# Attention heads: inverting the softmax sums in a reshaped copy, and scaling the results on GpSimd

## The chip, the cores and the metric

One core of a Trainium2 chip. The metric is the time of one execution on the device in microseconds (us), as a median over runs.

## The reference

1250 nodes with 768 features. A graph stage (two GAT layers over 41250 edges, added to the input) is followed by a transformer block: a layer norm, attention over all 1250 nodes with 12 heads of 64, and a mixture of 8 experts of which each node uses two. Everything is float32. The change lies in the attention alone:

```
qkv    = x @ Wqkv                      # 12 heads of 64
scores = q @ k.T * 64**-0.5            # 1250 x 1250 for each head
attn   = softmax(scores)               # exp(s - max) / sum
out    = (attn @ v) @ Wproj
```

## The kernel before

The graph stage, the attention, the projection with routing, and the experts follow each other. The attention runs over 18 *units*: 6 pairs of heads (`p`) times 3 chunks of 417, 417 and 416 queries (`k`). It works on transposed scores: keys on 125 partitions (10 key tiles, `j` = 0 to 9), queries along the free dimension, the two heads of the pair side by side, so that one tile `s` is 125 x 2 x 417.

For a unit, in the order of the data:
- `scores` (L674): TensorE makes the scores of one key tile for both heads (`st`, L678), ScalarE copies them to SBUF (`sT`, L681), VectorE folds them into a running maximum (`most`, L687).
- `top` (L689) and `row` (L698): TensorE transposes the maxima (`ptop`, L694), VectorE reduces them (`m`, L696), and TensorE spreads the result over the partitions (`mb`, L703).
- `weights` (L706): VectorE subtracts the maximum (L708), ScalarE takes the exponential (L709), GpSimd adds the exponentials of the key tiles up in `acc` (L714, two buffers).
- `values` (L716): TensorE multiplies the exponentials with `v` into `pav` (L722): 128 partitions (two heads of 64) by 417 queries.
- `divide` (L733): TensorE sums `acc` over the partitions with a matrix of ones (`pz`, L731), so that all 64 partitions of a head hold the same row of 417 sums. VectorE takes the reciprocal of the whole 128 x 417 tile (`rz`, L737) and multiplies `pav` by it into `aT` (L738).

Units overlap. In the loop (L756 to L788) unit `u` goes through `weights` and `values` while the next unit `nxt` goes through `scores`; the sums of the unit before (`last.divide()`, L769) stand between `u.top()` and `u.row()`. While a pair of heads runs, TensorE also computes the queries and keys of the next pair, in small steps put between the other work (`queries_keys`, L626; matmuls L641, evictions to `qk` by ScalarE, L644). For the last pair there is no next one: units 15, 16 and 17 have no such steps. I call units with such steps *filled*, and units 15 and 16 *plain*. Unit 17, the last, is filled up by the scheduler with the first matmuls of the projection (`po`, L929), and its sums are partly made on TensorE (`ns` = 5).

The order on TensorE inside a unit is as written (`manual_schedule`); the other engines' order is the scheduler's, and `keep_in_program_order` holds an instruction where it is written. Weights for the queries and keys (`wqk`, one buffer, 2 loads of 384 KB for a pair) come through SyncE's queue (L630): the load for the pair after next can only be issued when the last step has read the buffer. The same queue loads half of the rows `xs` (L155, L156) near the end of unit 14, and `first_w` (L843) at the end.

Of the kernel before, what the change touches and what calls it, by code (L numbers as in the profile page):

```python
# [10 lines left out]
F32 = mybir.dt.float32  # L11
# [6 lines left out]
ALU = mybir.AluOpType  # L18
# [9 lines left out]
def gnn_ffn_kernel(  # L28
# [24 lines left out]
    nc = tc.nc  # L53
    N, D = x.shape
    E = src.shape[0]
    P = 128
    T = 125
# [3 lines left out]
    H, HD = 12, 64  # L61
# [28 lines left out]
    CW = -(-N // NCK)  # L90
# [4 lines left out]
    small = ctx.enter_context(tc.tile_pool(name="small", bufs=3))  # L95
    dram = ctx.enter_context(tc.tile_pool(name="dram", bufs=1, space=bass.MemoryType.DRAM))
    keys = dram.tile([E + SL], F32, name="keys")
    xsd = dram.tile([N, D], F32, name="xsd")
    xd = dram.tile([NE * REG + P, RW], F32, name="xd")

    gate = ctx.enter_context(tc.tile_pool(name="gate", bufs=1))
# [61 lines left out]
    with tc.tile_pool(name="cnt", bufs=1) as cpool:  # L163
# [53 lines left out]
        with tc.tile_pool(name="edge", bufs=1) as ep, \  # L217
# [160 lines left out]
            for u0 in range(0, NU, 4):  # L378
                n = min(4, NU - u0)
# [224 lines left out]
    aT = attn.tile([P, DC, N], F32, name="aT")  # L604
    with tc.tile_pool(name="att", bufs=2) as ap, \
# [20 lines left out]
        def queries_keys(p):  # L626

            wqk = ap.tile([P, DC, 2, P], F32, tag="wqk", name="wqk", bufs=1)
            for i in (1, 0):
                nc.sync.dma_start(wqk[:, :, i, :], Wqkv[:, i * D + p * P:i * D + (p + 1) * P].rearrange(  # L630
                    "(c p) f -> p c f", p=P))
            qk = ap.tile([P, 2, N], F32, tag="qk", name="qk")
            yield qk
            for c0, w in CHUNKS:
                for i in (1, 0):
                    if i == 1:
                        pq = apm.tile([P, 2, 512], F32, tag="mb", name="pk")[:, 0, :]
                    else:
                        pq = apa.tile([P, 512], F32, tag="pz", name="pq")
                    for c in range(DC):  # L640
                        nc.tensor.matmul(pq[:, :w], wqk[:, c, i, :], yT[:, c, c0:c0 + w],  # L641
                                         start=(c == 0), stop=(c == DC - 1))
                        if c == DC - 1:
                            nc.scalar.mul(qk[:, i, c0:c0 + w], pq[:, :w], 1.0 if i == 1 else HD ** -0.5)  # L644
                        yield None

        def go(steps, n):
            for _ in range(n if steps is not None else 0):
                next(steps, None)
# [12 lines left out]
        onesf = ap.tile([T, HD], F32, name="onesf", bufs=1)  # L662
        nc.vector.memset(onesf, 1.0)

        class Unit:


# [38 lines left out]
            def weights(self, j):  # L706
                w, s = self.w, self.s[j]
                nc.vector.tensor_tensor(s[:, :, :w], s[:, :, :w], self.mb[:T, :, :w], ALU.subtract)  # L708
                nc.scalar.activation(s[:, :, :w], s[:, :, :w], AF.Exp)  # L709
                if j == 1:  # L710
                    self.acc = ap.tile([T, 2, CW], F32, tag="acc", name="acc")
                if 0 < j < self.ns:
                    prev = self.s[0] if j == 1 else self.acc
                    nc.gpsimd.tensor_tensor(self.acc[:, :, :w], prev[:, :, :w], s[:, :, :w], ALU.add)  # L714
# [15 lines left out]
                for i, r in enumerate(heads):  # L730
                    nc.tensor.matmul(self.pz[r, :self.w], onesf, t[:, i, :self.w], start=start, stop=stop)  # L731

            def divide(self):  # L733
                w = self.w
                self.sums(self.acc, self.ns == NT, True)
                rz = ap.tile([P, CW], F32, tag="rz", name="rz", bufs=1)
                nc.vector.reciprocal(rz[:, :w], self.pz[:, :w])  # L737
                nc.vector.tensor_tensor(aT[:, self.p, self.c0:self.c0 + w], self.pav[:, :w], rz[:, :w], ALU.mult)  # L738

        steps = queries_keys(0)  # L740
        qks = [next(steps)]
# [11 lines left out]
                    value_rows(j + BEFORE)  # L753
        units = [(p, k) for p in range(DC) for k in range(NCK)]
        steps = last = None
        for n, (p, k) in enumerate(units):  # L756
            if k == 0:
                steps = None
                if p + 1 < DC:
                    steps = queries_keys(p + 1)  # L760
                    qks.append(next(steps))
            nxt = Unit(*units[n + 1], qks[units[n + 1][0]]) if n + 1 < len(units) else None
            u.ns = NT if nxt is not None else NS
            with tc.manual_schedule(engines={mybir.EngineType.PE}):

                go(steps, 2)
                u.top()
                if last is not None:
                    last.divide()  # L769
                go(steps, DC - 2)  # L770
                if nxt is not None:
                    nxt.scores(0)
                u.row()
                u.weights(0)
                u.weights(1)
                for j in range(0, NT, 2):
                    for i in range(2):
                        if nxt is not None and j + i > 0:
                            nxt.scores(j + i)
                    if j < 6:  # L780
                        go(steps, 2)
                    for i in range(2):
                        if j + i + 2 < NT:
                            u.weights(j + i + 2)
                    for i in range(2):
                        u.values(j + i)
            last, u = u, nxt
        last.divide()  # L788


    pin = tc.keep_in_program_order
# [47 lines left out]
    def load_expert(w, w1s, w2s):  # L839

        w1 = w[:, :DC * FF].rearrange("p (c f) -> p c f", c=DC)
        w2 = w[:, DC * FF:].rearrange("p (c f) -> p c f", c=FC)
        nc.sync.dma_start(w1, w1s)  # L843
        nc.sync.dma_start(w2, w2s)
        return w1, w2

    def expert(e):
        return W1[e].rearrange("(c p) f -> p c f", p=P), W2[e].rearrange("(c p) f -> p c f", p=P)
# [60 lines left out]
    with tc.tile_pool(name="proj", bufs=3, reuse_waits="tile") as pp, \  # L909
# [6 lines left out]
        w = load_expert(first_w, *expert(0))  # L916
# [8 lines left out]
        def product(t):  # L925
            po = ppo.tile([P, 2, 512], F32, tag="po", name="po")
            for s in range(2):
                for c in range(DC):
                    nc.tensor.matmul(po[:T, s, :DH], aT[:, c, t * T:(t + 1) * T],  # L929
                                     wp[:, c, s * DH:(s + 1) * DH],  # L930
                                     start=(c == 0), stop=(c == DC - 1))
                    yield None
            y2 = pp.tile([T, D], F32, tag="y2", name="y2")
            ln_apply(y2, xs[:, t, :], st0[:, 0, t:t + 1], st0[:, 1, t:t + 1])
            o = y2.rearrange("p (s d) -> p s d", s=2)
            nc.vector.tensor_tensor(o, o, po[:T, :, :DH], ALU.add)
            mean, rstd = ln_stats(y2)
            yn = normed[t % len(normed)]
            ln_apply(yn[:T, :D], y2, mean, rstd)
            nc.vector.tensor_add(xs[:, t, :], xs[:, t, :], y2)  # L940
            split_rows(nc.sync if t % 2 == 0 else nc.scalar, out[t * T:(t + 1) * T, :], xs[:, t, :])
            nc.vector.tensor_copy(yn[:T, D:D + 1], number[:, t:t + 1])
            yield yn
# [106 lines left out]
        with tc.manual_schedule(engines={mybir.EngineType.PE}):  # L1050
            a, b = route(NT - 3, yns[NT - 3], tally), product(NT - 1)
# [9 lines left out]
            a, b = (route(t, yns[t], tally) for t in (NT - 2, NT - 1))  # L1061
# [17 lines left out]
    with tc.tile_pool(name="moe", bufs=2, reuse_waits="tile") as mp, \  # L1079
# [41 lines left out]
        for i, (e, n, _, _) in enumerate(jobs):  # L1121
# [6 lines left out]
            if i + 1 < len(jobs):  # L1128
                _, m, ws, slots = jobs[i + 1]
                xr, _ = fetch(slots(), m, pin)  # L1130
                w = load_expert(mp.tile([P, 2 * DC * FF], F32, tag="w", name="we"), *ws)
# [34 lines left out]
```

## Time and profile before

| | us |
|---|---|
| median of 3 runs | 1517.28 (1515.45 to 1519.91) |
| the profiled execution | 1518.66, its span 1516.8 |
| TensorE busy in the span | 1437.4 (95%) |
| VectorE busy | 808.4 (53%) |
| ScalarE, GpSimd busy | 574.4 (38%), 418.4 (28%) |
| reciprocals `rz` (L737) | 18 of 2.76 |
| multiplications into `aT` (L738) | 18 of 0.59 |
| units 0 to 14 end at | 1106.5 |
| unit 15, unit 16 | 1106.47 to 1133.27, 1133.27 to 1159.39 |

The time from one `ptop` to the next is taken as a unit. In a listing by time each line has the start, the time from the first to the last instruction of the group, the engine, the line, the operation, output and input, and the number of instructions; in brackets the idle time of the engine before it and what ended that. PEld is TensorE's weight load, which overlaps its matmuls. A window's row has, for each engine, the busy time and the instructions in it, then the TensorE clock that was granted, the share of the DMA engines' time, and GB/s.

### The profile page before, as it was taken

The page shows a single profiled execution, that of the slowest core. Times are in us where ns is not written, and L with a number is a line of the kernel's source. Part 1 is how long each engine was busy: PE and PEld are TensorE (multiplying, and loading weights), DVE is VectorE, ACT ScalarE, POOL GpSimd, SP SyncE. Part 2 cuts the span into 40 slices and gives each one's busy share as a digit, 9 for nine tenths or more (in the row PEclk, how much of TensorE's full clock was granted, in tenths as well). Part 3 has the DMA queues.
Part 4 walks back from the last instruction along what each step waited for, and adds up shares of the span by engine and source line. Part 5 has one row for each costly group of instructions (what it writes and reads, how often), then busy time and mean ns, then how long its engine had stood idle before and what let it go on. Part 6 is the DMA issues. An engine that isn't in the chain of part 4 may idle for free. (4 is left out here: it accounts for less than half of the span.)

```text
span 1516.8 us, 15936 instructions
## 1 busy us (share of the span) xinstructions
PE 1437.4 (95%) x5990; PEld 784.6 (52%) x5990; DVE 808.4 (53%) x1287; ACT 574.4 (38%) x915; POOL 418.4 (28%) x278
## 2 busy tenths in 40 slices
PE   6787999999999999999999999999988999899997
PEld 4574555556555555553343344344333666665654
DVE  6688456434036650127778778777878654111111
ACT  4220613205116521226646656655656223221211
POOL 5000000000000010006656655665666222222222
PEclk9758999999999999999999999999999998899999
DMA  7000020000021129940000000000030323565653
GB/s 208 22 2 11 11 73 0 0 28 5 3 100 42 60 81 383 373 152 0 22 1 0 22 1 21 1 22 0 4 99 1 134 107 136 215 234 171 229 187 124
DMA packets 48198, 124.58 MB, mean 82 GB/s; under 512 B 5629, under 2 KB 22207, under 8 KB 48120
## 3 DMA queue, kind: packets, MB, share of 16 engines
q1 hardware_dynamic: 31468, 57.35, 11.6%
q0 software_dynamic: 11968, 56.21, 10.2%
q10 hardware_dynamic: 4684, 9.99, 2.2%
q8 instruction: 48, 0.79, 0.2%
q14 instruction: 30, 0.25, 0.0%
HBM read 70.46 MB, written 57.55 MB: 84 GB/s over the span
## 5 line engine op out<-in xcount | busy, mean ns | idle before, releaser
L714 POOL TENSOR_TENSOR acc<-acc,sT 125x834 f32<-125x834 f32 (+1 forms) x139 | 272.9, 1963 | 10.9
L526 PE MATMUL pagg<-h,wt 125*125 125x385 f32 (+1 forms) x800 | 263.5, 486 | 0.4 <-DVE wt L519 0.4
L687 DVE TENSOR_TENSOR most<-most,st 125x834 f32<-125x834 f32 (+1 forms) x144 | 146.9, 1020 | 107.1 <-ACT sT L681 104.2
L526 PEld LDWEIGHTS pagg<-h,wt 125*125 125x125 f32 x800 | 147.0, 187 | 104.7 <-DVE wt L519 3.5
L708 DVE TENSOR_TENSOR sT<-sT,mb 125x834 f32<-125x834 f32 (+1 forms) x180 | 174.1, 1014 | 22.6 <-PE mb L703 22.6
L709 ACT ACTIVATE sT<-sT 125x834 f32<-125x834 f32 (+1 forms) x180 | 158.4, 900 | 49.3 <-DVE sT L708 48.9
L681 ACT COPY sT<-st 125x834 f32<-125x834 f32 (+1 forms) x180 | 151.6, 848 | 53.9 <-PE st L678 52.1
L678 PE MATMUL st<-qk 64*125 64x417 f32 (+1 forms) x720 | 164.8, 558 | 4.0 <-DVE most L687 4.0
L722 PE MATMUL pav<-sT,v 125*64 125x417 f32 (+1 forms) x720 | 151.8, 534 | 9.4 <-ACT sT L709 9.4
L619 POOL MEMSET zero<- 128x771 f32 x1 | 0.7, 740 | 529.7 <-PE ptr L143 529.7
L714 POOL TENSOR_TENSOR acc<-sT 125x834 f32<-125x834 f32 (+1 forms) x18 | 35.4, 1964 | 275.9 <-ACT sT L709 275.9
L678 PEld LDWEIGHTS st<-qk 64*125 64x125 f32 x720 | 56.8, 185 | 99.4 <-issue 43.2
L722 PEld LDWEIGHTS pav<-sT,v 125*64 125x64 f32 x720 | 42.8, 137 | 106.3 <-issue 44.4
L900 PE MATMUL poe<-we,hT 128*128 128x384 f32 x264 | 89.8, 486 | 0.0
L641 PE MATMUL pq<-yT,wqk 128*128 128x417 f32 (+1 forms) x216 | 88.1, 534 | 0.0
L867 PE MATMUL phe<-xT,we 128*128 128x384 f32 (+1 forms) x288 | 86.6, 460 | 0.0
L929 PE MATMUL po<-wp,aT 128*125 128x384 f32 x240 | 86.5, 497 | 0.0
L641 PE MATMUL pk<-yT,wqk 128*128 128x417 f32 (+1 forms) x216 | 84.0, 526 | 0.0
L206 PE MATMUL ph<-gw,xnT 128*125 128x384 f32 x240 | 81.6, 500 | 0.8 <-DMA gw<-in_L_gnn_W_dram 0.8
L657 PE MATMUL pv<-wv,yT 128*125 128x384 f32 x240 | 79.9, 490 | 1.4 <-issue 1.4
L206 PE MATMUL ph<-gw,x1T 128*125 128x384 f32 x240 | 79.2, 491 | 0.0
L530 DVE RECIPROCAL rz<-pagg 125x1 f32<-125x1 f32 x20 | 3.3, 166 | 141.4 <-PE pagg L526 141.4
(225 smaller groups left out, 1718.5 us busy)
## 6 DMA issues: line engine op xcount, KB each, us to landing
xd<-zero POOLq DMA_DIRECT2D x8, 3855.0 KB, 15.7
we<-in_L_ffn_W_dram SPq DMA_DIRECT2D x16, 1152.0 KB
xr<-xd SPq DMA_DIRECT2D x25, 385.5 KB
gw<-in_L_gnn_W_dram SPq DMA_DIRECT2D x2, 2304.0 KB
wqk<-in_L_ffn_Wqkv_dram SPq DMA_DIRECT2D x12, 384.0 KB
xres<-in_x_dram SPq DMA_DIRECT2D x10, 375.0 KB
xsd<-xres ACTq DMA_DIRECT2D x10, 375.0 KB
xn<-in_x_dram SPq DMA_DIRECT2D x9, 336.0 KB
```

The lines of the kernel that those rows point to most:

```text
L206: nc.tensor.matmul(po[:, s, :DH], xT[:, c, t * T:(t + 1) * T], w[:, c, s * DH:(s + 1) * DH], start=(c == 0), stop=(c == DC - 1))
L526: nc.tensor.matmul(po[:, s, :DH + s], ws[j][:, (d - d0) * T:(d - d0 + 1) * T], h[:, j, s * DH:(s + 1) * DH + s], start=(j == 0), stop=(j = ...
L641: nc.tensor.matmul(pq[:, :w], wqk[:, c, i, :], yT[:, c, c0:c0 + w], start=(c == 0), stop=(c == DC - 1))
L678: nc.tensor.matmul(st[:T, i, :w], self.qk[r, 1, j * T:(j + 1) * T], self.qk[r, 0, self.c0:self.c0 + w], start=True, stop=True)
L681: nc.scalar.copy(s[:, :, :w], st[:T, :, :w])
L687: nc.vector.tensor_tensor(self.most[:, :, :w], prev[:, :, :w], st[:T, :, :w], ALU.max)
L708: nc.vector.tensor_tensor(s[:, :, :w], s[:, :, :w], self.mb[:T, :, :w], ALU.subtract)
L709: nc.scalar.activation(s[:, :, :w], s[:, :, :w], AF.Exp)
L714: nc.gpsimd.tensor_tensor(self.acc[:, :, :w], prev[:, :, :w], s[:, :, :w], ALU.add)
L722: nc.tensor.matmul(self.pav[r, :w], v[:, j, hd0:hd0 + HD], s[:, i, :w], start=(j == 0), stop=(j == NT - 1))
L867: nc.tensor.matmul(ph[:, :n * P], w1[:, c, f * P:(f + 1) * P], xT[:, c, :], start=(c == 0), stop=(c == DC - 1))
L900: nc.tensor.matmul(po[:, d, :DH], hT[:, f, s * P:(s + 1) * P], w2[:, f, d * DH:(d + 1) * DH], start=(f == 0), stop=(f == FC - 1))
```

## The change

For 17 of the 18 units, `divide` no longer divides. ScalarE copies the sums to SBUF (`zs`) and the unscaled results to `aT`. Two DMAs write one row of 417 sums for each head to memory (`zd`, padded to 420), and one reads the 840 values back as 120 partitions of 7 columns (`z`). VectorE inverts that tile in the middle of the next unit (`invert`, pinned after the block `j == 4`). One DMA writes the inverses to memory (`zr`), two spread them over 64 partitions each (`rz`, two buffers). At the top of the unit after that, GpSimd multiplies `aT` by `rz` in place (`scale`, pinned). The last unit still divides as before. `acc` gets one buffer in place of two.

```diff
+    ZW = 420
+    zd = dram.tile([3 * H // 2, 2, ZW], F32, name="zd")
+    zr = dram.tile([3 * H // 2, 2, ZW], F32, name="zr")
...
+        zs = ap.tile([P, ZW], F32, name="zs", bufs=1)
+        nc.vector.memset(zs, 1.0)
+        ZQ = 7
+        ZP = 2 * ZW // ZQ
+
+        def inverses(n):
+            return ap.tile([P, ZW], F32, tag="rz", name="rz")
...
-                    self.acc = ap.tile([T, 2, CW], F32, tag="acc", name="acc")
+                    self.acc = ap.tile([T, 2, CW], F32, tag="acc", name="acc", bufs=1)
...
-            def divide(self):
+            def divide(self, n):
                 w = self.w
                 self.sums(self.acc, self.ns == NT, True)
-                rz = ap.tile([P, CW], F32, tag="rz", name="rz", bufs=1)
-                nc.vector.reciprocal(rz[:, :w], self.pz[:, :w])
-                nc.vector.tensor_tensor(aT[:, self.p, self.c0:self.c0 + w], self.pav[:, :w], rz[:, :w], ALU.mult)
+                self.o = aT[:, self.p, self.c0:self.c0 + w]
+                if n + 1 == len(units):
+                    nc.vector.reciprocal(zs[:, :w], self.pz[:, :w])
+                    nc.vector.tensor_tensor(self.o, self.pav[:, :w], zs[:, :w], ALU.mult)
+                    return
+                nc.scalar.copy(zs[:, :w], self.pz[:, :w])
+                nc.scalar.copy(self.o, self.pav[:, :w])
+                for i in range(2):
+                    nc.sync.dma_start(zd[n, i:i + 1, :], zs[i * HD:i * HD + 1, :])
+                self.z = small.tile([ZP, ZQ], F32, tag="z", name="z", bufs=1)
+                nc.sync.dma_start(self.z, zd[n].rearrange("i (a b) -> (i a) b", b=ZQ))
+
+            def invert(self, n):
+                tc.keep_in_program_order(nc.vector.reciprocal(self.z, self.z))
+                nc.sync.dma_start(zr[n].rearrange("i (a b) -> (i a) b", b=ZQ), self.z)
+                self.rz = inverses(n)
+                for i in range(2):
+                    nc.sync.dma_start(self.rz[i * HD:(i + 1) * HD, :], zr[n, i:i + 1, :].to_broadcast([HD, ZW]))
+
+            def scale(self):
+                tc.keep_in_program_order(nc.gpsimd.tensor_tensor(self.o, self.o, self.rz[:, :self.w], ALU.mult))
...
+        waiting = []
...
                 if last is not None:
-                    last.divide()
+                    last.divide(n - 1)
+                for old in waiting:
+                    old.scale()
...
                     for i in range(2):
                         u.values(j + i)
+                    if j == 4 and last is not None:
+                        last.invert(n - 1)
+                        waiting = [last]
             last, u = u, nxt
-        last.divide()
+        last.divide(n)
+        for old in waiting:
+            old.scale()
```

## The prediction

> **What bounds the kernel now.** TensorE is busy for 95% of the span, so I first asked where in the attention it is not. Windows of about one unit each:
>
> ```profile
> 819.00:848.00 29.00, 28.69 (x127) 11.82 (x128) 22.76 (x23) 17.09 (x22) 17.64 (x9) 1.00 0.10 28
> 1107.00:1130.00 23.00, 19.73 (x86) 6.96 (x84) 20.26 (x20) 14.98 (x18) 14.70 (x9) 0.85 0.29 76
> 1130.00:1152.00 22.00, 17.87 (x84) 6.82 (x84) 19.13 (x20) 13.64 (x17) 13.00 (x8) 0.92 0.00 1
> ```
>
> The third number is TensorE, the fifth group VectorE. A filled unit has 28.69 of 29 us on TensorE; what is left is one wait of 0.31 for an exponential. In the plain units TensorE is idle for 3 to 4 us of 22, VectorE is busy for 87 to 88%, and the granted clock is below 1.
>
> Next, what the reciprocal holds up. In a filled unit (VectorE's listing by time):
>
> ```profile
> 820.16 2.76 DVE L737 RECIPROCAL rz<-pz 128x417 f32<-128x417 f32 x1
> 822.95 0.59 DVE L738 TENSOR_TENSOR aT<-pav,rz 128x417 f32<-128x417 f32 x1
> 824.90 2.88 DVE L708 TENSOR_TENSOR sT<-sT,mb 125x832 f32<-125x832 f32 x3 [1.36 <-PE mb L703]
> ```
>
> Both are done 1.36 us before the first subtraction can start, which waits for `mb`, behind TensorE's six steps: they cost nothing there. In unit 15, from the listing of all engines:
>
> ```profile
> 1108.72 2.75 DVE L737 RECIPROCAL rz<-pz 128x416 f32<-128x416 f32 x1
> 1109.24 1.12 PE L703 MATMUL mb<-ident,m 105*125 105x105 f32 x8
> 1111.39 0.96 DVE L708 TENSOR_TENSOR sT<-sT,mb 125x834 f32<-125x834 f32 x1
> 1112.27 0.58 DVE L738 TENSOR_TENSOR aT<-pav,rz 128x416 f32<-128x416 f32 x1
> 1113.34 1.03 PE L722 MATMUL pav<-sT,v 125*64 125x417 f32 x4 [2.08 <-ACT sT L709]
> 1116.35 3.15 PE L678 MATMUL st<-qk 64*125 64x417 f32 x8
> 1119.10 1.02 DVE L687 TENSOR_TENSOR most<-most,st 125x834 f32<-125x834 f32 x1 [0.66 <-ACT sT L681]
> ```
>
> Here `mb` ends at 1110.36 and the subtraction starts at 1111.39: the reciprocal is late. TensorE waits 2.08 us for the first exponential, and then the matmuls of two score tiles take 3.15 us (1.67 in the filled unit), because the clock has fallen:
>
> ```profile
> 1107.00:1114.00 7.00, 4.92 (x30) 2.30 (x28) 6.39 (x6) 2.81 (x4) 0.03 (x1) 1.00 0.93 247
> 1114.00:1121.00 7.00, 6.61 (x20) 2.13 (x20) 6.34 (x8) 5.30 (x7) 5.98 (x4) 0.51 0.01 2
> 1141.00:1145.00 4.00, 3.49 (x12) 1.34 (x12) 4.00 (x5) 2.33 (x4) 3.32 (x2) 0.57 0.01 4
> ```
>
> **What it removes.** 17 reciprocals of 2.76 and 17 multiplications of 0.59 leave VectorE, 57 us of work. In units 1 to 14 they end 1.36 us early, so the gain is 0. Unit 17: after `mb` TensorE runs without a gap (projection matmuls fill it), so 0. Units 15 and 16: with no reciprocal the first subtraction starts about 0.10 after `mb` (as 824.90 against 824.80), at 1110.46 instead of 1111.39: 0.93. The multiplication held 0.50 more between subtractions (1112.27 to 1112.76). Together 1.43 a unit; in unit 16 the same rows read 1138.20, 1139.08 and 1139.58, again 1.43. Two units: 2.86. What follows (exponential, `pav`, the next scores, their copies, the maxima) is a ring in which each waits for the link before, so I let it all move up.
>
> **The clock.** TensorE's idle of 2.08 shrinks to about 1.2, since the first exponential can start at 1111.5, not 1112.38 (in the built order it now also stands ahead of the second score copy). If the clock then stays up, VectorE's idle behind the slow scores goes too: 0.66 above and 0.63 at the same place in unit 16, 1.29 in all. If it falls anyway, 0. Nothing in the trace shows a gap of 1.2 us in a stretch this thin, so I take half, 0.65.
> The Trainium skill, page "TensorE: Matmul & The Clock Gate", section "What's actually happening", has the clock halve only after a whole idle window of about 3.4 us. By that rule a gap of 2.08 would leave it at 1.00 and this term would be 0. The trace shows 0.51 after it; the trace decides.
>
> **What it adds to VectorE.** One reciprocal of 120x7 in the middle of each unit. One-column reciprocals (L132) took 145 to 166 ns, and 417 columns 2758, so 6.6 ns a column: 0.16 to 0.20. In filled units VectorE has idle time at the end of the unit; in the two plain ones it costs 0.4. It waits for `z`, and the unit's last two subtractions are queued behind it. In a filled unit `pz` ends at 819.86; a copy (0.52, the row of L644), two issues (0.46 each, L630), a landing, an issue and a landing lead to `z`. The rows nearest to such small transfers are the indirect ones, 3.1 us to memory and 4.8 from it:
>
> ```profile
> sofar<-out_dram,ids POOLq DMA_INDIRECT x23, 4.8
> out_dram<-sofar,ids POOLq DMA_INDIRECT x23, 3.1
> ```
>
> With 4.8 for both, 831.4; the slot, after the first of three subtractions at 834.23, is 835.2. Covered. In unit 15 the `xs` loads fill the DMA engines until about 1114, so `z` comes at 1118 to 1120, close to its slot at 1120: 0 to 1 us, taken as 0.
>
> **ScalarE** gets two copies of about 0.52 ahead of the `qk` eviction and the first score copy. They wait for `pav` and `pz`, during an idle of 6.93 (filled) and 4.43 (unit 15): 0, and 1.0 if that cover were gone. In unit 15 the `xs` DMA issues stand between them; the first exponential needs its subtraction (1111.42) anyway.
>
> **GpSimd** gets 17 multiplications; 834 columns take 1.96, so 417 about 1.0. They stand before a unit's first addition, where it is idle for 10.6 (filled) or 7.8 (plain), and `rz` landed in the unit before: 0. The chain of nine additions starts with the second exponential and so moves up with it; in unit 16 it ended at 1159.90 and `pz` began at 1160.43, a margin of 0.53. Unit 16's own multiplication comes at about 1177, ahead of the projection tile that needs it (after 1185). `acc` with one buffer: the next first addition (828.47) waits for matmuls that ended at 819.86: 0.
>
> **SyncE** gets 102 DMAs. What is queued behind them: `wqk` at four pair changes, `xs` in unit 14, `first_w` in unit 17 (issued 1179.43, `rz` before that). For `wqk`, from three views (SyncE's queue, windows of 1 us, weight loads):
>
> ```profile
> 837.33 0.96 SPq L630 DMA_DIRECT2D wqk<-in_L_ffn_Wqkv_dram  x2
> 840.00:841.00 1.00, 1.00 (x8) 0.33 (x6) 0.26 (x1) 1.00 (x2) 0.92 (x2) 1.00 1.15 333
> 841.00:842.00 1.00, 1.00 (x8) 0.15 (x4) 0.90 (x2) 0.49 (x1) 1.00 (x1) 1.00 0.34 85
> 845.39 0.30 PEld L641 LDWEIGHTS pk<-yT,wqk 128*128 128x128 f32 x2 [0.65 <-issue]
> ```
>
> Both halves are in by about 841.3, the half needed first by about 840.2, and it is used at 845.39. Now the queue waits for the write of `zr`, then issues two `rz`: 835.4 (slot and reciprocal) + 0.46 + landing 3.1 + 0.92 = 839.9, 2.5 late; with 4.8, 4.2 late. The `rz` themselves move 215 KB, 0.65 at 333 GB/s. The first half is then in by 843.4 to 845.1: hidden at both ends, and I take 0.
> [...]
>
> TensorE's work is unchanged; in unit 17 six instead of nine projection matmuls stand ahead of `pz`, a change of order in a stretch without gaps: 0.
>
> **Sum.** 2.86 + 0.65 - 0.4 = 3.1 us. The profiled execution would go from 1518.66 (span 1516.8 and 1.9 around it) to 1515.6. It was 1.4 above the median of the runs, so I take the gain off the median: 1517.28 - 3.1 = 1514.2.
>
> **Rivals.** What this kernel's measurement can tell from no change is about 0.3%, 4.55 us: below 1512.7 is faster, above 1521.8 slower.
> - *The clock stays up and the later waits shrink too.* In the two units TensorE also waits 2.5 us for `most` before scores and 1.0 before `ptop`. Gain 2.86 + 1.29 - 0.4 = 3.75 and half of these 3.5: 5.5, time 1511.8. For it: the falls of the clock follow the gap. Against: those waits come from the copy and maximum latencies, which stay.
> - *The ring does not move.* The clock falls as before and scores, not VectorE, set the pace: gain 0, 1517.3. Against: TensorE's wait of 2.08 is for VectorE.
> - *The load of `wqk` comes too late* (slower). If the 120 short pieces of `zr` take longer than 5.1 us to land (845.39 less 840.2 and 0.65 leaves 4.5 of lateness), TensorE waits at each of four pair changes. It outweighs the gain and 0.3% when 4 x late = 3.1 + 4.55, late by 1.9, a landing of 7.0 us. At 8 us: 4 x 2.9 - 3.1 = +8.5, 1525.8. Against: no row of a small DMA above 4.8.
> - *It does not do what it says:* the built order still has the wide reciprocal once, in unit 17 (idle 6.64 before it, no gap on TensorE), so this one is out.
>
> **Numbers.** Forecast case 0.58, larger gain 0.22, ring not moving 0.06, late `wqk` (or an additional wait of 0.55 in each of fourteen filled units, which would weigh as much) 0.14. Faster 0.22, same 0.64, slower 0.14. The range takes in the larger gain (1511.8) and the ring that does not move (1517.3), each with about half the spread that the three runs showed (4.5): 1509.8 to 1519.6.
>
> **What would show it.** Right: filled units still 28.92 us apart, 28.69 of 29 busy; in units 15 and 16 the first subtraction 0.1 after `mb`, and the two units together 2.5 to 3.8 shorter than 52.92. Wrong: a weight load of `pk` that waits for a DMA, VectorE idle before the reciprocal of `z`, or plain units no shorter.

## The result and the profile after

Over 20 runs each the changed kernel took 1515.32 us and the kernel before 1517.35 (medians). The recorded ratio is 0.9993 with a 95% interval of 0.9982 to 1.0005 (the two medians alone would give 0.9987): no difference that this measurement can tell. The forecast was 1514.2 in a range of 1509.8 to 1519.6, with "same" as the likeliest. A second comparison (12 runs against 28) gave 1516.47 against 1516.74, 0.9997 (0.9980 to 1.0014). Two single runs far above all others, 1900.75 us of a version tested below and 3317.81 us of the kernel before, are left out of the ratios.

The unit's steps have other line numbers in the changed kernel: `ptop` is L705, `pz` L742, `st` L689, `mb` L714, the subtraction L719, the exponential L720, `most` L698, `pav` L733, `acc` L725, the copy of scores L692. New are the copies `zs` L753 and `aT` L754, the DMAs `zd` L756, `z` L758, `zr` L762, `rz` L765, the small reciprocal L761 and GpSimd's multiplication L768. The page's head:

```profile
span 1513.5 us, 16154 instructions
PE 1431.7 (95%) x5990; PEld 782.7 (52%) x5990; DVE 756.8 (50%) x1271; ACT 590.3 (39%) x949; POOL 435.2 (29%) x295
```

The profiled execution took 1515.23. VectorE lost 51.6 us of work (808.4 to 756.8), ScalarE gained 15.9 and GpSimd 16.8, and the span is only 3.3 shorter. Windows of the filled unit and of two stretches of unit 15 (third number TensorE, fifth group VectorE's, then the granted clock):

```profile
820.00:849.00 29.00, 28.69 (x127) 11.82 (x128) 19.57 (x22) 18.12 (x24) 18.51 (x10) 1.00 0.14 36
1107.00:1114.00 7.00, 4.80 (x28) 2.63 (x28) 4.04 (x5) 2.46 (x4) 2.07 (x2) 1.00 1.04 242
1114.00:1121.00 7.00, 5.17 (x26) 1.73 (x28) 7.00 (x9) 6.49 (x10) 4.93 (x3) 1.00 0.23 63
```

In the filled unit VectorE has 3.2 us less to do and TensorE's 28.69 of 29 has not moved. In unit 15 the clock stays at 1.00 where it was 0.51. The rows of unit 15 that answer to those shown of before:

```profile
1111.05 1.12 PE L714 MATMUL mb<-ident,m 105*125 105x105 f32 x8
1112.28 2.89 DVE L719 TENSOR_TENSOR sT<-sT,mb 125x834 f32<-125x834 f32 x3 [1.67 <-PE mb L714]
1114.29 0.92 PE L733 MATMUL pav<-sT,v 125*64 125x417 f32 x4 [1.22 <-ACT sT L720]
1116.68 1.67 PE L689 MATMUL st<-qk 64*125 64x417 f32 x8
```

The first subtraction now waits for `mb` (1111.05 + 1.12 = 1112.17, started at 1112.28), TensorE's gap is 1.22 instead of 2.08, and two score tiles take 1.67 instead of 3.15. The filled unit and SyncE's queue at a pair change:

```profile
825.90 2.88 DVE L719 TENSOR_TENSOR sT<-sT,mb 125x832 f32<-125x832 f32 x3 [4.66 <-PE mb L714]
836.16 0.19 DVE L761 RECIPROCAL z<-z 120x7 f32<-120x7 f32 x1
```

```profile
836.38 0.32 SPq L762 DMA_DIRECT2D zr<-z  x1
837.85 1.09 SPq L765 DMA_DIRECT2D rz<-zr  x2
839.04 1.12 SPq L633 DMA_DIRECT2D wqk<-in_L_ffn_Wqkv_dram  x2
846.39 0.30 PEld L644 LDWEIGHTS pk<-yT,wqk 128*128 128x128 f32 x2 [0.65 <-issue]
```

VectorE's idle before the subtraction grew from 1.36 to 4.66, nothing else. The small reciprocal runs without a wait, and `pk` does not wait for its weights.

Where the time went, stage by stage (one profile each; nearly all that the change touches lies in the last column but one, below called the stretch):

| | first `ptop` | unit 14 | unit 15 | unit 16 | `ptop` to `mb`, unit 17 | `ptop` of unit 1 to `mb` of unit 17 | from there to the end |
|---|---|---|---|---|---|---|---|
| before | 672.97 | 28.19 | 26.80 | 26.12 | 2.40 | 459.42 | 355.0 |
| after | 673.98 | 29.02 | 24.83 | 24.16 | 2.80 | 456.69 | 353.4 |
| after less before | +1.0 | +0.83 | -1.97 | -1.96 | +0.40 | -2.73 | -1.6 |

The first and the last column are stages whose code is the same. Two losses in the stretch were not foreseen. The one in unit 14, from the listing of all engines (ACTq is ScalarE's queue):

```profile
1104.78 0.30 ACTq L159 DMA_DIRECT2D xs<-xsd  x1
1105.18 0.85 ACT L692 COPY sT<-st 125x834 f32<-125x834 f32 x1 [2.41 <-DMA xs<-xsd]
1108.28 1.10 PE L705 MATMUL ptop<-ident,most 125*105 125x125 f32 x8 [1.54 <-DVE most L698]
```

and the same issue and copy in the kernel before:

```profile
1102.71 0.30 ACTq L156 DMA_DIRECT2D xs<-xsd  x1
1103.37 0.85 ACT L681 COPY sT<-st 125x834 f32<-125x834 f32 x1 [1.59 <-PE st L678]
```

A copy of scores stands behind an issue of an `xs` load in ScalarE's queue, and that issue waits until an earlier load is through. `ptop` of the two kernels stands 0.98 apart at the start of unit 14; less that, the issue comes 1.09 later than before and the copy 0.83 later: the whole 0.83. Ahead of the first `xs` load on SyncE the queue now has `zr` and two `rz` (1096.65 to 1099.19); that load goes out at 1099.29, 0.64 later than before by the same base.

The loss in unit 17, first before, then after:

```profile
1143.64 16.26 POOL L714 TENSOR_TENSOR acc<-acc,sT 125x834 f32<-125x834 f32 x8
1160.43 0.92 PE L731 MATMUL pz<-acc,onesf 125*64 125x417 f32 x4
1161.79 1.12 PE L703 MATMUL mb<-ident,m 105*125 105x105 f32 x8 [0.44 <-DVE m L696]
```

```profile
1142.90 16.27 POOL L725 TENSOR_TENSOR acc<-acc,sT 125x834 f32<-125x834 f32 x8
1159.22 0.92 PE L742 MATMUL pz<-acc,onesf 125*64 125x417 f32 x4 [0.85 <-POOL acc L725]
1160.07 1.12 PE L714 MATMUL mb<-ident,m 105*125 105x105 f32 x8
```

GpSimd's nine additions took 18.3 us in both kernels. They began 8.33 after `ptop` of unit 16 (1141.60) and now 7.75 (1140.86), 0.58 earlier; the unit became 1.96 shorter. 1.96 - 0.58 - the margin of 0.53 = 0.85, the wait in the row. Before, TensorE waited 0.44 for `m` ahead of `mb`; that wait is gone, which leaves the loss of 0.40.

### The profile page after: what moved, and what is told of

It is laid out like the page before. It is cut to its first block, busy times and chain, and to the rows that moved or that the text cites. A ratio compares the mean times of both kernels' runs of the same rounds, so it can differ in the third digit from the quotient of the medians.

```text
span 1513.5 us, 16154 instructions
## 1 busy us (share of the span) xinstructions
PE 1431.7 (95%) x5990; PEld 782.7 (52%) x5990; DVE 756.8 (50%) x1271; ACT 590.3 (39%) x949; POOL 435.2 (29%) x295
## 5 line engine op out<-in xcount | busy, mean ns | idle before, releaser
L725 POOL TENSOR_TENSOR acc<-acc,sT 125x834 f32<-125x834 f32 (+1 forms) x139 | 272.9, 1963 | 10.9
L719 DVE TENSOR_TENSOR sT<-sT,mb 125x834 f32<-125x834 f32 (+1 forms) x180 | 174.5, 1013 | 73.9 <-PE mb L714 73.9
L698 DVE TENSOR_TENSOR most<-most,st 125x834 f32<-125x834 f32 (+1 forms) x144 | 147.0, 1021 | 105.5 <-ACT sT L692 102.2
L720 ACT ACTIVATE sT<-sT 125x834 f32<-125x834 f32 (+1 forms) x180 | 158.1, 900 | 43.5 <-DVE sT L719 43.0
L692 ACT COPY sT<-st 125x834 f32<-125x834 f32 (+1 forms) x180 | 151.3, 848 | 42.3 <-PE st L689 38.0
L689 PE MATMUL st<-qk 64*125 64x417 f32 (+1 forms) x720 | 162.5, 551 | 5.3 <-DVE most L698 5.2
L733 PE MATMUL pav<-sT,v 125*64 125x417 f32 (+1 forms) x720 | 149.5, 527 | 8.0 <-ACT sT L720 8.0
L725 POOL TENSOR_TENSOR acc<-sT 125x834 f32<-125x834 f32 (+1 forms) x18 | 35.3, 1963 | 256.5 <-ACT sT L720 256.5
L689 PEld LDWEIGHTS st<-qk 64*125 64x125 f32 x720 | 55.9, 182 | 98.8 <-DVE most L698 52.5
L733 PEld LDWEIGHTS pav<-sT,v 125*64 125x64 f32 x720 | 42.4, 135 | 103.7 <-issue 42.8
```

What stands on the lines that cost most here:

```text
L689: nc.tensor.matmul(st[:T, i, :w], self.qk[r, 1, j * T:(j + 1) * T], self.qk[r, 0, self.c0:self.c0 + w], start=True, stop=True)
L692: nc.scalar.copy(s[:, :, :w], st[:T, :, :w])
L698: nc.vector.tensor_tensor(self.most[:, :, :w], prev[:, :, :w], st[:T, :, :w], ALU.max)
L733: nc.tensor.matmul(self.pav[r, :w], v[:, j, hd0:hd0 + HD], s[:, i, :w], start=(j == 0), stop=(j == NT - 1))
```

## Experiments

My theory after the first comparison: the gain is made in units 15 and 16 alone, part of it VectorE's work and part the clock, and the two losses take back 1.2 us. The rivals: filled units gain or lose too; the clock has nothing to do with the change; the difference is what two profiles of one kernel show anyway.

Where no rounds are named, a kernel was run once. Such a time says little (single runs of the kernel before lay between 1511.27 and 1523.25); what the run tells is read from the stages of its profile.

**The kernel before, profiled again** (no edit).

> The kernel before, once more, for a second profile of it. If the fall of the TensorE clock depends on when the idle of 2.08 us comes within windows that run freely, this profile may have it in one, both or none of the plain units, which then take about 26.8 (two cold windows), 26.1 (one) or 25.9 us (none, worked out from the rows at full clock). If the fall belongs to the gap alone, both units again take 26.8 and 26.1.

1516.82. Unit 14 28.19 again, unit 15 25.58 and unit 16 25.83, the stretch 457.88: 1.54 less than in the first profile of the same code, 1.51 of it in units 15 and 16. There the clock fell for one stretch of 3.4 us in each unit. The granted clock over the two units was 0.87 and 0.93 in the first profile, 0.93 and 0.93 in the second. So of the 3.93 that the first pair of profiles shows there, up to 1.5 was how the clock fell in one of them.

**The new path for the plain units alone** (sums of units 14 to 16; the old reciprocals of the first two stood in units 15 and 16):

```diff
+        PLAIN = (DC - 1) * NCK
...
-                if n + 1 == len(units):
+                if n + 1 == len(units) or n < PLAIN - 1:
...
-                    if j == 4 and last is not None:
+                    if j == 4 and n >= PLAIN:
```

> The change is kept for the sums of units 14 and 15 alone, whose division stood in the plain units 15 and 16; units 0 to 13 divide as before. I measure the stretch from the ptop of unit 1 to the mb of unit 17 (459.42 us before, 456.69 after). Theory (only the plain units pay for the reciprocal): filled units 28.92 as in both, plain units 24.8 and 24.2 as after, stretch 456.7. Rival (the filled units gain or lose by the chain through memory, hidden in the sum): the stretch differs from 456.7 by over 0.5. Total time as after, within the spread of the runs.

**The new path for the filled units alone** (sums of units 0 to 13):

```diff
+        PLAIN = (DC - 1) * NCK
...
-                if n + 1 == len(units):
+                if n >= PLAIN - 1:
...
                 for old in waiting:
                     old.scale()
+                waiting = []
...
-                    if j == 4 and last is not None:
+                    if j == 4 and 0 < n < PLAIN:
```

> The other half: units 0 to 13 go through memory, units 14 and 15 divide as before in the plain units. Theory: nothing is gained in fourteen units, though 14 reciprocals of 2.76 us leave VectorE; plain units about 26 to 26.8 us as before (less where the clock happens to stay up), stretch 457.6 to 459.4. Rival (gain in the filled units): stretch below 457, filled units shorter than 28.92.

Five rounds each. Plain units alone: 1514.77 against 1518.37, ratio 0.9979 (0.9964 to 0.9995), the only interval of all that lies below 1. Units 15 and 16 at 24.83 and 24.15, as with the whole change, and unit 14 at 28.20: no loss there. The stretch was 455.90, 0.8 below the 456.7 expected, and by its own rule (over 0.5) the rival holds: a filled unit does lose by the path through memory, unit 14. Filled units alone: 1520.04 against 1518.37, ratio 1.0010 (0.9995 to 1.0024). Filled units (2 to 13) 28.91 to 28.94 as before, unit 14 at 29.25, units 15 and 16 at 25.64 and 25.78 (the second profile of before: 25.58, 25.83). So 14 of the 17 reciprocals were moved for nothing, and the loss in unit 14 comes with them: their `zr` and `rz` stand ahead of the `xs` loads. In the version for plain units ScalarE's copy waited 1.59, as before, instead of 2.41.

**A second reciprocal in the filled units** of the kernel before, to see how far the cover reaches:

```diff
-            def divide(self):
+            def divide(self, twice=False):
...
                 nc.vector.reciprocal(rz[:, :w], self.pz[:, :w])
+                if twice:
+                    nc.vector.reciprocal(rz[:, :w], self.pz[:, :w])
...
-                    last.divide()
+                    last.divide(n < (DC - 1) * NCK)
```

> Before, with the reciprocal done twice in the filled units (once in the plain ones). It was early by 1.36 us, so 2.76 more should be 1.4 late. Theory (the cover is 1.36 and then VectorE is in the way): filled units 0.7 to 1.5 us longer than 28.92, TensorE waits for exponentials. Rival (TensorE has other work and hides all of it): 28.92.

1531.02. Filled units (1 to 13) went from 28.92 to 29.70: 2.76 of work added, 0.79 of time. Unit 14, with the `xs` loads, went from 28.19 to 30.63; a copy of scores waits 2.01 there for an `xs` load, and what makes up the rest is open. In another filled unit:

```profile
854.64 2.75 DVE L737 RECIPROCAL rz<-pz 128x416 f32<-128x416 f32 x1
857.42 2.76 DVE L739 RECIPROCAL rz<-pz 128x416 f32<-128x416 f32 x1
858.16 1.12 PE L703 MATMUL mb<-ident,m 105*125 105x105 f32 x8
860.10 0.96 DVE L708 TENSOR_TENSOR sT<-sT,mb 125x834 f32<-125x834 f32 x1
860.98 0.58 DVE L740 TENSOR_TENSOR aT<-pav,rz 128x416 f32<-128x416 f32 x1
```

`mb` there ended at 859.28 (858.16 + 1.12), so the subtraction is 0.82 late, and that is the price. It is less than the 1.4 expected because the multiplication now comes behind the first subtraction: 2.76 - 1.36 - 0.59 = 0.81. One reciprocal is hidden and a second is not: what removing one would bring is 0, and the listing of before had said so with its 1.36.

This run showed something else, which I had not asked of it. Its plain units are those of the kernel before, and the clock did not fall in them, with the same gap in unit 15 (2.07) and one of 1.84 in unit 16:

```profile
1120.71:1146.05 25.34, 20.11 (x100) 7.42 (x101) 22.38 (x22) 16.57 (x20) 16.39 (x9) 1.00 0.23 60
1146.05:1171.46 25.41, 20.17 (x101) 7.42 (x101) 22.45 (x22) 16.48 (x20) 17.68 (x10) 1.00 0.00 1
```

```profile
1127.58 0.92 PE L722 MATMUL pav<-sT,v 125*64 125x417 f32 x4 [2.07 <-ACT sT L709]
```

So units 15 and 16 with the old division took 52.92, 51.41, 51.42 (filled units alone) and 50.75, by how often the clock fell.

**The clock held up in the kernel before**: four matmuls of 417 columns for each unit, whose result nothing uses, put into TensorE's gap of the plain units.

```diff
+                    if j == 0 and steps is None and nxt is not None:
+                        fill = apa.tile([P, 512], F32, tag="pz", name="fill")
+                        for r in heads + heads:
+                            nc.tensor.matmul(fill[r, :last.w], onesf, last.acc[:, 0, :last.w], start=True, stop=True)
                     for i in range(2):
                         u.values(j + i)
```

> Before, with four more matmuls of 417 columns into the bank of pz in the two plain units, in TensorE's gap ahead of the first pav, on data that is there; nothing uses their result. VectorE's work is that of before, reciprocal included. Theory (half of the gain is the clock): the gap shrinks to under 0.6, the granted clock stays at 1.00, plain units 25.5 to 26.0 instead of 26.80 and 26.12. Rival (the gain is VectorE's alone): no shorter than before.

1517.05. Windows of units 15 and 16:

```profile
1105.73:1131.06 25.33, 21.72 (x108) 7.90 (x108) 22.38 (x22) 16.56 (x20) 16.92 (x10) 1.00 0.29 73
1131.06:1156.46 25.40, 21.79 (x109) 7.91 (x109) 22.44 (x22) 16.48 (x20) 17.66 (x10) 1.00 0.00 1
```

and the same two of the changed kernel:

```profile
1108.28:1133.11 24.83, 19.84 (x101) 7.50 (x101) 19.45 (x21) 17.13 (x23) 17.36 (x10) 1.00 0.33 82
1133.11:1157.27 24.16, 20.16 (x101) 7.41 (x101) 19.42 (x21) 17.21 (x22) 17.76 (x11) 1.00 0.04 10
```

With a clock of 1.00 and the wide reciprocal in place the two units take 50.73 (50.75 above, where nothing was added to them and the clock did not fall); without the reciprocal 48.99. The difference, 1.74, is what VectorE's work was worth. The rest of the gain is the clock: 52.92 - 50.73 = 2.19 against the first profile of before, 51.41 - 50.73 = 0.68 against the second.

**The changed kernel with a wide reciprocal put back** in the plain units, on a tile that nothing uses:

```diff
+        held = ap.tile([P, CW], F32, name="held", bufs=1)
+        nc.vector.memset(held, 1.0)
...
                 for old in waiting:
                     old.scale()
+                if steps is None and nxt is not None:
+                    pin(nc.vector.reciprocal(held, held))
```

> After, with a reciprocal of 128x417 on a scratch tile put on VectorE behind the reduction in the two plain units, so that it holds up the first subtraction as the old one did; nothing uses its result. Theory: the first subtraction 0.93 later against mb, TensorE's gap back to about 2.1, plain units 0.9 longer than 24.83 and 24.16 at full clock, and 1.5 to 2 longer where the clock falls. Rival (the gain is from the copies on ScalarE and the scaling on GpSimd, which are still there): plain units stay at 24.8 and 24.2.

1516.71. Unit 16, with its clock at 1.00, took 24.90, 0.74 more than without. Unit 15 took 25.73; its clock fell for one stretch (0.59 in the row of that window), so its 0.90 is not VectorE's alone; with a fall 1.5 to 2 had been expected. Unit 16 shows the reciprocal's price at full clock, 0.74 of the 1.24 that the unit gained against the version with the clock held up (25.40 to 24.16). The other 0.50 would be the multiplication, which was not put back; that is argued, not tested. `ptop` to `mb` in unit 17 went back to 2.39: with longer units GpSimd is in time again.

**All `xs` loads on SyncE:**

```diff
-            split_rows(nc.sync if t % 2 == 0 else nc.scalar, xs[:, t, :], xsd[t * T:(t + 1) * T, :])
+            split_rows(nc.sync, xs[:, t, :], xsd[t * T:(t + 1) * T, :])
```

> After, with all loads of xs issued by SyncE, none by ScalarE. Theory (the loss at the end of unit 14, 29.02 instead of 28.19 from ptop to ptop, is score copies that stand on ScalarE behind an xs load which waits for a free transfer): unit 14 back to 28.2, stretch 0.8 shorter, 455.9. Rival (it is the traffic itself, or GpSimd): 29.0 as after.

1520.65 (before beside it 1521.42). Unit 14 is back at 28.19, so the loss there needs the issue in ScalarE's queue. Unit 15 became 24.06 and unit 16 24.93; their sum is 48.99, to the hundredth that of the changed kernel. The 0.77 only changed places: the scheduler's order of the last copies in unit 15 differs, and the first subtraction of unit 16 then waits 2.56 for `mb` instead of 1.79.

**GpSimd's chain one addition shorter in unit 16** (TensorE sums one tile more directly):

```diff
-            u.ns = NT if nxt is not None else NS
+            u.ns = NT - 1 if n + 2 == len(units) else NT if nxt is not None else NS
```

> After, with the last addition of unit 16 taken from GpSimd: its tenth tile of exponentials is summed by two matmuls. Theory (in the shorter unit GpSimd's chain of additions ends last and holds pz by 0.85): from the ptop to the mb of unit 17 2.4 instead of 2.80, stretch 0.4 shorter, 456.3. Rival (pz waits for its own bank or for ScalarE): 2.8 as after.

1516.72. `ptop` to `mb` in unit 17 is 2.39, unit 16 24.30 (0.14 more). Unit 17 in that kernel:

```profile
1159.84 0.92 PE L742 MATMUL pz<-acc,onesf 125*64 125x417 f32 x4
1161.20 1.12 PE L714 MATMUL mb<-ident,m 105*125 105x105 f32 x8 [0.44 <-DVE m L707]
```

No wait for `acc`; what ends the wait for `mb` is again VectorE's `m`. The loss of 0.40 was GpSimd's chain.

**Both losses taken away**: plain units alone and the shorter chain, and the same with all `xs` loads on SyncE; beside them the changed kernel once more. Five rounds, one chip.

> The path through memory for the sums of units 14 and 15 alone, and GpSimd's chain of additions one tile shorter in unit 16 (TensorE takes that tile's column sums instead). If the two losses have the causes named so far, unit 14 stays at 28.2 us, units 15 and 16 at 24.83 and 24.2 to 24.3, and the way from ptop to mb in unit 17 goes back from 2.80 to 2.40: the whole stretch from ptop of unit 1 to mb of unit 17 is 455.90 - 0.40 + 0.15 = 455.6 us, 3.8 below the first profile of the kernel before and 2.3 below its second. In the time of the kernel: ratio to before 0.9975 to 0.9985. Rival: what is saved in the stretch is lost in the variation of the other stages, and the ratio is no different from that of the version without the shorter chain (0.9979), its interval taking in 1.

> As the version before it in this call, and all xs loads issued by SyncE instead of every second one by ScalarE. With the path through memory gone from units 1 to 13, no small DMA stands ahead of the xs loads, so one theory expects nothing from this: unit 14 at 28.2 and the stretch within 0.3 us of the version before it. Rival: the issues on ScalarE still delay the copies of unit 15, as in the listing where unit 15 became 24.06 instead of 24.83 with all of them on SyncE; then unit 15 is 0.8 shorter, but unit 16 was 0.8 longer there, so the sum would be the same.

> The changed kernel once more, to see what of its numbers stays in a second profile. If the windows of the clock run freely, the granted clock in units 15 and 16 may fall in this profile though it was 1.00 in the first; if a gap of 1.22 us in TensorE never costs the clock, the two units are 24.83 and 24.16 again. Losses that come from the order of the work stay in both cases: unit 14 at 29.0 and 2.8 from ptop to mb in unit 17. Ratio to before 0.9993 as in the comparison shown, within 0.001.

| | unit 14 | unit 15 | unit 16 | `ptop` to `mb`, unit 17 | stretch | median | ratio to before |
|---|---|---|---|---|---|---|---|
| plain units, shorter chain | 28.19 | 25.58 | 24.15 | 2.40 | 456.20 | 1517.69 | 1.0011 (0.9994 to 1.0027) |
| and `xs` on SyncE | 28.18 | 24.06 | 25.07 | 2.39 | 455.58 | 1518.20 | 1.0009 (0.9993 to 1.0026) |
| changed kernel again | 29.01 | 24.83 | 24.16 | 2.80 | 456.68 | 1516.47 | 0.9997 (0.9980 to 1.0014) |

Both losses are gone, as expected, and the stretch with `xs` on SyncE is the shortest of all. In the time of the kernel nothing of it shows: the expected ratio of 0.9975 to 0.9985 was missed, the rival's interval that takes in 1 came, neither version beats the kernel before by what can be told, and the 0.9979 of the version for plain units did not come back with the shorter chain. So I call no version better. The changed kernel's stretch came out the same to 0.01 us, and its spans were 1513.5 and 1510.5: the 3.0 lie ahead of the attention (first `ptop` at 673.98 and 670.95).

The first of these versions also missed its number in unit 15, 25.58 instead of 24.83, and the windows say why:

```profile
1109.30:1112.71 3.41, 1.57 (x10) 0.40 (x8) 3.41 (x5) 3.00 (x4) 0.43 (x1) 1.00 0.49 151
1112.71:1116.12 3.41, 3.41 (x12) 1.17 (x8) 3.41 (x4) 2.13 (x4) 3.33 (x2) 0.51 0.02 1
1116.12:1119.53 3.41, 3.16 (x18) 1.07 (x16) 3.41 (x6) 3.41 (x5) 3.25 (x3) 0.99 0.00 0
```

```profile
1110.66 0.92 PE L734 MATMUL pav<-sT,v 125*64 125x417 f32 x4 [1.22 <-ACT sT L721]
1112.20 1.13 PE L734 MATMUL pav<-sT,v 125*64 125x417 f32 x4 [0.62 <-ACT sT L721]
1113.26 3.11 PE L690 MATMUL st<-qk 64*125 64x417 f32 x8
```

TensorE's gaps are those of the changed kernel, 1.22 and 0.62. Here both fell into one stretch of 3.41 us before the fall, in which TensorE was busy for 1.57 (46%), and the clock was halved for the next 3.41. In six other profiles of unit 15 with these gaps (the changed kernel twice, plain units alone, the shorter chain alone, and both versions with `xs` on SyncE) it was not.

Why the same gap costs the clock in one profile and not in another can be read from the traces. Within a profile the clock changed only at times that lie whole multiples of 3.41 us apart, so these clock stretches (each much shorter than the stretch of the tables) can be counted on from one change to the next. In units 15 and 16 of the thirteen profiles the clock fell eight times, each time behind a clock stretch in which TensorE was busy for 31 to 46%. One other stretch at 46% kept 1.00, and all the rest were at 48% or more (the least busy of unit 15 in the six profiles just named at 57 to 64%). The gap of 2.08 in the first profile of before lay in one stretch (first row); with the doubled reciprocal the border between two stretches cut the gap of 2.07 (the other rows):

```profile
1110.61:1114.02 3.41, 1.33 (x8) 0.20 (x4) 3.41 (x5) 1.97 (x3) 0.00 (x0) 1.00 0.83 224
```

```profile
1123.09:1126.50 3.41, 2.42 (x16) 1.24 (x12) 3.41 (x2) 1.71 (x2) 0.00 (x0) 1.00 0.95 241
1126.50:1129.92 3.42, 1.83 (x10) 0.46 (x10) 3.42 (x6) 1.80 (x2) 0.89 (x1) 1.00 0.02 5
```

An estimate from these numbers: at 46% a stretch holds 1.84 us of idle. A gap of 2.08 puts so much into one stretch for 1.81 of the 3.41 us of positions that it can have, about half; the two gaps of the changed kernel, 2.76 from the start of the first to the end of the second, for 0.65 of 3.41, about a fifth. Seen were six of eight with the old division (seven of ten with the version, tested above, that puts a reciprocal back) and one of seven.

## Why the prediction held, and where it did not

**Filled units, 0.** Right for units 2 to 13: 28.90 to 28.94 in every profile with the old reciprocal or without it, and 0.79 for a second one. Unit 14 is taken up below.

**Plain units, VectorE: 2.86 - 0.4.** The start was right in kind: `mb` now ends the wait, and unit 16 gained 1.24 against the version with the clock held up, where the terms give 0.93 + 0.50 - 0.2 = 1.23. Unit 15 gained only 0.50 (25.33 to 24.83). The step that failed is "so I let it all move up". VectorE's work fell by 2.93 there (22.38 to 19.45), and its idle time rose by 2.43, from 2.95 to 5.38; that is 0.65 more than in unit 16 (2.96 to 4.74). One place of it, from VectorE's listing of the changed kernel:

```profile
1130.90 2.15 DVE L698 TENSOR_TENSOR most<-most,st 125x834 f32<-125x834 f32 x2 [1.42 <-ACT sT L692]
```

With the other waits of this kind (0.77 and 0.21) the maxima at the end of the unit wait 2.40 for ScalarE's copies, against 0.77 + 0.80 + 0.19 = 1.76 in the version with the clock held up. The 2.46 of the sum was 1.74.

**The clock, half of 1.29.** The step that failed is that the fall after a gap of 2.08 was taken as certain and its price as fixed. With gaps of 1.84 to 2.09 the two units with the old division lost 2.17, 0.66, 0.67 and 0 to the clock (52.92, 51.41, 51.42, 50.75, less 50.75); with a gap of 1.22 unit 15 lost 0.75 once in seven profiles. What the change does is to make a fall rarer, not to remove it, and the term has no one value: 2.19 against the first profile of before, 0.68 against the second. What decides is how much of TensorE's idle time falls into one stretch of 3.41 us, and that differs from one execution of a program to the next.
The Trainium skill, page "TensorE: Matmul & The Clock Gate", section "What's actually happening", says that the window is free-running and does not start with the kernel, and gives its length as 3413 ns. The runs agree: the halved stretch above is 3.41 long, and the same code shows other falls in other profiles. That a whole idle window is needed they do not bear out: TensorE was busy for 46% of the one before the fall, and for 31 to 39% of those before the seven others.

**ScalarE, 0, and SyncE, 0.** The prediction listed `xs` in unit 14 among what is queued behind the new DMAs on SyncE, and then priced `wqk` alone. That is the step left out: +0.83. I had looked at ScalarE's issues of `xs` only in unit 15, and there for the new copies. What a delayed transfer on one queue does to an issue on another, and to the copies behind it, was in none of the terms.

**GpSimd, 0.** Wrong by 0.40. "The chain starts with the second exponential and so moves up with it" was true, but its end is compared with the end of a unit that moved up by 1.96 while its start moved by 0.58. A margin of 0.53 is safe only as long as the unit shrinks by no more than that beyond the chain's own start.

**`wqk`, 0.** Right, with the lateness overpriced: the issue at 839.04 is 838.04 on the time base of before, 0.7 later than 837.33, not 2.5 to 4.2. The term that was too large is the landing: `zr` was issued at 836.38 and `rz` followed at 837.85, so 1.47 from issue to landing where rows of other DMAs gave 3.1 to 4.8. All 17 of them, and the way of the sums to `z`, from the queue's waits (us in total, times, longest):

```profile
SPq L765 <- DMA zr<-z: 19.3, 17, 2.1
SPq L758 <- DMA zd<-zs: 17.5, 17, 3.5
```

1.14 and 1.03 on average, behind issues of 0.32 and about 0.5; the longest, 3.5, is unit 15's, which ran beside the `xs` loads and still reached its slot.
The Trainium skill, page "DMA: Bandwidth & Descriptors", section "Anatomy of one DMA", gives a fixed cost of about 2.0 us for DMAs from GpSimd's queue. For these, from SyncE's queue, 1.47 was measured.

**The sum.** In the stretch, against the first profile of before: -1.74 (VectorE) - 2.19 (clock) + 0.83 (unit 14) + 0.40 (unit 17) = -2.70, measured -2.73. Against the second: -1.74 - 0.68 + 0.82 + 0.41 = -1.19, measured 457.88 to 456.69, -1.19. The forecast of -3.1 came near the first of them through errors that cancel: VectorE too high by 0.72, the clock too low by 1.54, 1.23 of losses missing. That is luck, and the range of 9.8 us would have held an unchanged time too, so the time of the kernel was no test of the mechanism. The ratio of the runs says -1.1 us (-2.7 to +0.8), which is nearer to the smaller figure and excludes neither; that the larger was partly an unlucky profile to start from is shown by the second profile of before, not by the runs.

**The rivals.** The larger gain (5.5) did not come: the later waits for `most` stayed. A ring that does not move is out (1.74 at a constant clock). `wqk` never came late. An additional wait in the filled units came, but in one of them (0.83 in unit 14), not in fourteen.

What stays open is why versions with a shorter stretch were not faster over the runs. The stages that no version touches vary by more than the stretch does: over the profiles the first `ptop` came between 670.95 and 678.61, and from `mb` of unit 17 to the end it took 352.4 to 356.3. The two versions with all `xs` on SyncE had the latest first `ptop` (677.77, 678.61); their loads of `xn` at the very start ran late (a block of twelve issues on SyncE took 20.7 and 20.8 us; in the other kernels 14.7 to 19.1). Whether that is chance or comes with the program was not settled.

## What to carry to other kernels

Before moving work off an engine, read in each stage what the next step on it waits for: where the listing shows it waiting for another engine after the work is done (1.36 us here, in 14 of 17 cases), moving it buys nothing, and its replacement still costs queue places. When a stage shrinks, every chain of fixed length that must end in it (GpSimd's additions) has to be set against the new length, and every queue that new DMAs enter has to be followed to the last waiter, across to the compute instructions behind an issue on another engine. And before a difference of 0.2% is explained, profile the unchanged kernel more than once: its two plain units alone differed by 1.5 us between two profiles, and by 2.2 from those of the profile in which the clock stayed up.

## What the runs showed of the hardware

- The clock falls by stretches of 3.41 us that do not start with the work. In units 15 and 16 of thirteen profiles it fell behind stretches with TensorE busy for 31 to 46% and kept 1.00 behind one of 46% and all of 48% and more. So a gap of 2.07 kept 1.00 where a border of two stretches cut it (71% and 54%), and gaps of 2.08 and 2.09, each within one stretch, cost 2.17 us in two units.
- A DMA issue in ScalarE's queue that had to wait for an earlier transfer held up the copies behind it, by 2.41 us of ScalarE's idle time in one place.
- A write of 3 KB from SyncE to memory was through 1.47 us after its issue began; GpSimd's multiplications of 128 x 417 took 0.92 to 1.08, and ScalarE's copies of that size 0.51.
